# A graph layer on one core: half of the last block's tiles scattered into a matrix in the table stage, and shorter fills behind the scatters

## The chip, the cores and the metric

The kernel runs on one NeuronCore of a Trainium2 chip. The metric is the device time of one execution in microseconds (us). The time before is 271.71 us, the median of 3 runs (271.37 to 273.13). The engines are named as in the profile: PE is TensorE (matmul), PEld its weight load, DVE VectorE, ACT ScalarE, POOL GpSimd, SP SyncE. A q behind a name (SPq, ACTq) is an engine's instruction queue, from which DMAs are issued.

## The reference

One relational graph layer on 625 nodes of 512 features and 20,625 edges, sorted by destination. Each edge belongs to one of four relations and has a weight. In short:

```python
h = max(layernorm(x), 0)
total_msg = sum_r (h[src] @ W_rel[r] + b_rel[r]) * where(edge_type == r, edge_weight, 0)
agg = segment_sum(total_msg, dst) / max(segment_sum(edge_weight, dst), 1)
x1 = layernorm(h + h @ W_self + b_self + agg) * ln1_g + ln1_b
ffn = gelu(x1 @ W_ffn1 + b_ffn1) @ W_ffn2 + b_ffn2
out = x + layernorm(x1 + ffn) * ln2_g + ln2_b
```

All of it is float32.

## The kernel before

**Blocks and tiles.** The nodes lie in five blocks of up to 128 rows (`NB` = 5, the second has 113). The edges lie in 162 tiles of 128. From the counts alone (not the values) `EdgePlan` derives for each tile a window of rows in which its destinations must lie; a tile whose window leaves its block is kept for a slow way at the end, which counts show to be unused. Blocks 0 and 4 are the outer ones (`OUTER`): 31 tiles (0 to 30) lie wholly in block 0, and 32 (130 to 161) wholly in block 4.

**Table stage.** In 20 steps (4 relations by 5 blocks) `table_rows` makes the message of every node under every relation: eight matmul instructions a step on PE (L385), an eviction on DVE (L398), a store to the tensor `table` in HBM (L400). Some of these chunks stay on chip. Around the steps stand other works, each pinned to a step by a constant: the columns of the edges, one-hots for the degrees (`DEGREE_HOTS_AT`), the residual adds (`ADDS_AT`), the first hots for the banks (`HOTS_AT`). The order on PE, DVE, ACT and POOL is that of the program text.

**Edges of the outer blocks without gathers.** The tiles that lie wholly in an outer block are not gathered. Their contribution is a product: a matrix `sums_w[b]` of 128 nodes by 20 chunks by 128 rows holds the summed weights from each table row to each node of the block, and PE multiplies it with the 20 chunks of the table (`chunk_sum`, L1249). The matrix is made in two ways:

- Block 0, by scatter. The tiles' edges are loaded as a line with 63 neighbours on each side (`line`, L250). `line_columns` makes keys and places; `line_sums`, called for a piece of up to eight columns at the steps `COLUMNS_AT`, compares each edge with its neighbours (L639), keeps the first of each equal key and adds the weights of the others to it (L641 to L647). For each column, `scatter` then writes 128 weights to cells of the HBM tensor `cells`, cleared before (L256), with an indirect DMA on POOL (L653), and a memset (L656, 400 elements) as a fill behind it. `PACE` says how many scatters may be in the program by each step. `load_sums` loads the matrix back on ACT's queue (L670) at step `LOAD_AT`.
- Block 4, by banks. For each tile of the 32, `node_hots` makes two one-hots on DVE (L552 for two tiles at once, L562), `weighted_hots` two weighted copies on ACT (L570), and `outer_sum` two matmuls (L584) into a bank of PSUM that covers 25 nodes. A full bank is added to the overlap with the bank before (`empty_bank`, L525), copied (L536) and laid into `sums_w[4]` (L537). Three groups of two tiles are made in the table stage (`HOTS_AT`), the rest in the edge stage.

**Edge stage.** All other tiles, 99 of them, are gathered: an indirect DMA on POOL per tile (`gather`, L1103), each with a fill of 200 elements behind it (L1106); six more (L1161) fetch the edges at the borders of blocks. Eight buffers `ms` take the rows. ACT and DVE weight and add the rows (L1110, L1128), PE sums them by a one-hot (L1153). Then come the first norm, the feed-forward (L884, L902) and the second norm, block by block. The order on the engines is computed by a small planner (`Plan`) from costs in us that are written with each operation, with time zero near the end of the table stage and POOL free at 3.9.

**Between the stages on POOL.** At step `FIRST_AT` = 15, `load_first_edges` issues three indirect loads (L765), which `first_columns` on DVE reads later. `after_stores` (L663) is a short memset that waits for all table stores but the last two and for all scatters; the first gather stands behind it and waits for the last stores as well.

Of the kernel before, what the change touches and what calls it, by code (L numbers as in the profile page):

```python
# [20 lines left out]
PIECE = 8  # L21


class EdgePlan:
# [41 lines left out]
    def row(self, node):  # L66
        return node + (self.gap if node >= self.gap_at else 0)

# [80 lines left out]
def gnn_layer(ctx, tc, x, edges, edge_line, edge_groups, w_self, w_rel, w_ffn1, w_ffn2, rows_in, bf1_in, out, n_edges):  # L149
# [86 lines left out]
    LB, LJ, LN = outer[0]  # L236
    WL = LN + 2 * NEAR + 1
    line = early.tile([P, 4, WL], I32, name="line")
    cells = dram.tile([P * NC * P + P * LN, 1], F32, name="cells")

    def load_rows(to, n0, n1):
# [8 lines left out]
    nc.sync.dma_start(line, bass.AP(tensor=edge_line.tensor, offset=edge_line.offset,  # L250
                                    ap=[[LN, P], [edge_line.shape[1], 4], [1, WL]]))
# [4 lines left out]
    nc.sync.dma_start(cells[:P * NC * P, :].rearrange("(p c n) o -> p c (n o)", p=P, n=D // 2),  # L256
                      zeros.bitcast(F32).unsqueeze(1).to_broadcast([P, 2 * NC * P // D, D // 2]))
    nc.sync.dma_start(ed, edges)
    load_wr(1)
    load_rows(brel_bc[:, D:], D, R * D)  # L260
    load_rows(rows, R * D, (R + 6) * D)

    def later_loads(r):
        if r == 0:
            load_wr(2)
            nc.sync.dma_start(ws_sb, w_self)
            nc.sync.dma_start(bf1, bf1_in)
        if r == 1:
            load_wr(3)
            nc.sync.dma_start(w1_sb, w_ffn1)  # L270
        if r == 2:
            nc.sync.dma_start(w2_sb, w_ffn2)
# [170 lines left out]
    def count_outside():  # L443
# [8 lines left out]
        def total():  # L452
            pcnt = buffer("ps")
            nc.tensor.matmul(pcnt[0:1, 0:1], cnt, ones, start=True, stop=False)
            nc.tensor.matmul(pcnt[0:1, 0:1], x_missing, ones, start=False, stop=False)
            for i in range(2):
                nc.tensor.matmul(pcnt[0:1, 0:1], far[:, i:i + 1], ones, start=False, stop=(i == 1))
            return lambda: nc.vector.tensor_copy(n_out, pcnt[0:1, 0:1])
# [4 lines left out]
    banked_blocks = outer[1:]  # L463
    NE = sum(n for _, _, n in banked_blocks)

    GW = D // NC
    outer_tiles = [(b, j) for b, j0, n in banked_blocks for j in range(j0, j0 + n)]
# [42 lines left out]
    def empty_bank(k):  # L510
# [12 lines left out]
        def added():  # L523
            if not starts_:
# [3 lines left out]
        def copied():  # L528
            if starts_:
                for a, e in ((0, n0 - b * P), (max(bk[2] for bk in bank_of if bk[0] == b) - b * P, P)):  # L530
                    for a_ in range(a, e, GW):
                        n = min(GW, e - a_)
                        nc.scalar.activation(sums_w[b][:, :, a_:a_ + n], key_row[:, :NC * n].rearrange(
                            "p (c n) -> p c n", c=NC), AF.Copy, scale=0.0)
# [41 lines left out]
    def outer_sum(k, k0, box):  # L576
# [4 lines left out]
        for part in range(2):  # L581
# [5 lines left out]
    far = const.tile([P, 2], F32, name="far")  # L587
    spill = early.tile([P, LN], F32, name="spill")
    nc.gpsimd.iota(spill, pattern=[[1, LN]], base=P * NC * P, channel_multiplier=LN,
                   allow_small_or_imprecise_dtypes=True)  # L590
    place, found, weight = (early.tile([P, LN], F32, name=name) for name in ("place", "found", "weight"))
    cell = early.tile([P, LN], I32, name="cell")
    line_f = early.tile([P, 3, WL], F32, name="line_f")
    line_key = early.tile([P, WL], F32, name="line_key")
    own_of_line = slice(NEAR, NEAR + LN)
# [5 lines left out]
    def line_columns():  # L601

        own = own_of_line
        up = early.tile([P, 2, WL], F32, name="line_up")
        nc.vector.tensor_copy(line_f, line[:, 0:3, :])
        nc.vector.tensor_scalar(up, line_f[:, 0:2, :], float(ep.gap_at), float(ep.gap), op0=ALU.is_ge, op1=ALU.mult)
        nc.vector.tensor_add(line_f[:, 0:2, :], line_f[:, 0:2, :], up)
        s, d, t = line_f[:, 0, :], line_f[:, 1, :], line_f[:, 2, :]
        nc.vector.scalar_tensor_tensor(t, t, float(NP), s, op0=ALU.mult, op1=ALU.add)
        nc.vector.scalar_tensor_tensor(line_key, t, 1024.0, d, op0=ALU.mult, op1=ALU.add)  # L610
        part = early.tile([P, LN], F32, name="line_s")
        at = early.tile([P, LN], F32, name="line_t")
        e, near = nc.gpsimd, 1.5 * 2.0 ** 23
        e.tensor_scalar(found, d[:, own], float(LB * P), None, op0=ALU.is_ge)
        e.tensor_scalar(at, d[:, own], float(LB * P + P), None, op0=ALU.is_lt)
        e.tensor_mul(found, found, at)
# [3 lines left out]
        e.tensor_scalar(place, s[:, own], float(NC * P - 1), None, op0=ALU.mult)  # L620
        e.tensor_add(place, place, d[:, own])
        e.tensor_add(place, place, t[:, own])
        e.tensor_scalar(part, part, float(P - P * NC * P), float(-LB * P), op0=ALU.mult, op1=ALU.add)
        e.tensor_sub(part, part, spill)
        e.tensor_add(place, place, part)

    def line_check():
        d = line_f[:, 1, :]
        junk = early.tile([P, 2, LN], F32, name="line_j")
        for i, at in enumerate((2 * NEAR + 1, NEAR + 1)):  # L630
            nc.vector.scalar_tensor_tensor(junk[:, i, :], d[:, own_of_line], 0.0, d[:, at:at + LN], op0=ALU.add,
                                           op1=(ALU.is_equal, ALU.is_gt)[i], accum_out=far[:, i:i + 1])

    def line_sums(k0, k1):

        n, at = k1 - k0, slice(k0, k1)
        same = early.tile([P, PIECE, 2 * NEAR + 1], F32, tag="same", name=f"same_{k0}", bufs=1)[:, :n, :]
        own = line_key[:, NEAR + k0:NEAR + k1].unsqueeze(2).to_broadcast([P, n, 2 * NEAR + 1])
        nc.vector.tensor_tensor(same, sliding(line_key, k0, n, 2 * NEAR + 1), own, op=ALU.is_equal)  # L639
        earlier = early.tile([P, PIECE], F32, tag="earlier", name=f"earlier_{k0}", bufs=1)[:, :n]  # L640
        nc.vector.reduce_sum(earlier, same[:, :, :NEAR], axis=mybir.AxisListType.X)  # L641
        nc.vector.scalar_tensor_tensor(earlier, earlier, 0.0, found[:, at], op0=ALU.is_equal, op1=ALU.mult)
        nc.vector.tensor_mul(earlier, earlier, place[:, at])
        nc.vector.tensor_add(cell[:, at], earlier, spill[:, at])
        nc.vector.tensor_tensor(same[:, :, NEAR:], same[:, :, NEAR:],
                                sliding(line[:, 3, :].bitcast(F32), NEAR + k0, n, NEAR + 1), op=ALU.mult)
        nc.vector.reduce_sum(weight[:, at], same[:, :, NEAR:], axis=mybir.AxisListType.X)  # L647

    scattered = []
    idle = const.tile([P, 2 * PAUSE], BF16, name="idle")  # L650

    def scatter(k):
        i = nc.gpsimd.indirect_dma_start(  # L653
            out=cells[:, :], out_offset=bass.IndirectOffsetOnAxis(ap=cell[:, k:k + 1], axis=0),
            in_=weight[:, k:k + 1], in_offset=None)
        nc.gpsimd.memset(idle, 0.0)  # L656
        if scattered:
# [861 lines left out]
```

## Time and profile before

| what | value |
|---|---|
| median of 3 runs | 271.71 us |
| the profiled execution's own time | 273.46 us |
| its span, first to last instruction | 271.7 us |
| granted TensorE clock, mean | 0.987 |
| POOL busy | 202.9 us (75%), 378 instructions |
| DVE busy | 197.4 us (73%), 481 instructions |
| ACT busy | 75.3 us (28%), 182 instructions |
| PE busy | 255.7 us (94%), 1075 instructions |

All times in the profile are of one execution. PE's ends are modelled, so its busy share overstates it. A row of the time line gives the start, the duration, engine and line, operation, what is written and read, and in brackets the idle time of the engine ahead of it with what ended it. A row of the groups gives the busy sum, the mean in ns and the idle time in front. The chain of waits follows the work that ended last backwards, at each step to what released it.

### The profile page before, as it was taken

The numbers are of one execution on the slowest core, as the hardware profiler recorded it, in microseconds if no ns is written. First come the engines' busy times: TensorE is split into PE (matmuls) and PEld (weight loads), VectorE is DVE, ScalarE is ACT, GpSimd is POOL, SyncE is SP. The second block draws the span as 40 slices with busy tenths as digits, with TensorE's granted clock in tenths as the row PEclk, the third lists the DMA queues.
The fourth block names the chain that finished last, engine by engine and source line by source line (L and its number), as shares of the span: only waits on it lengthen the run. The fifth ranks groups of instructions, "written<-read, shape, count | busy, mean of one in ns | idle before, by whom it ended". The sixth has DMA issues, their size and how long they took to land.

```text
span 271.7 us, 3653 instructions
## 1 busy us (share of the span) xinstructions
PE 255.7 (94%) x1075; PEld 146.0 (54%) x1075; DVE 197.4 (73%) x481; ACT 75.3 (28%) x182; POOL 202.9 (75%) x378
## 2 busy tenths in 40 slices
PE   7799999999999979997799999999999998999993
PEld 5344444544547435552444345585684964856972
DVE  2877999869675955984885689784599975957514
ACT  3010000000130753875522123142133341520420
POOL 4789999999931888998898898888889898841000
PEclk9999999999999999999689999999999999999999
DMA  6999998712172886789659985666666577660101
GB/s 189 356 425 420 382 394 311 247 46 73 43 273 78 246 293 185 238 286 304 197 163 309 341 294 162 185 183 183 188 194 186 171 215 226 185 179 0 41 0 42
DMA packets 21495, 57.28 MB, mean 211 GB/s; under 512 B 3889, under 2 KB 6449, under 8 KB 20450
## 3 DMA queue, kind: packets, MB, share of 16 engines
q0 software_dynamic: 9488, 27.57, 34.5%
q1 hardware_dynamic: 11696, 28.02, 28.1%
q10 hardware_dynamic: 290, 1.44, 1.4%
q8 instruction: 9, 0.15, 0.2%
q14 instruction: 12, 0.10, 0.1%
HBM read 49.17 MB, written 7.85 MB: 210 GB/s over the span
## 4 chain that ended last, share of the span: by engine, by line
PE 35%; POOL 24%; DMA 21%; DVE 11%; issue 4%; ACT 1%; SPq 1%; POOLq 0%; DVEq 0%; ACTq 0%
PE ps L385 22%; DMA ms<-table,row_i 18%; POOL ms L1103 17%; POOL zeros L1106 5%; PE ps L902 4%; PE ps L884 3%; DMA wr<-in_L_gnn_W_rel_dram 2%; PE acc L1153 2%; POOL ms L1161 2%; DVE add L1128 2%; DVE es L1128 2%; PE acc L1249 1%; DVE z L1045 1%; DVE xs L1047 1%; DVE el L1118 1%
## 5 line engine op out<-in xcount | busy, mean ns | idle before, releaser
L1103 POOL DMA_INDIRECT ms<-table,row_i x99 | 101.3, 1023 | 18.7 <-issue 12.1
L385 PE MATMUL ps<-wr,hT 128*128 128x512 f32 (+2 forms) x168 | 71.3, 577 | 1.5 <-DMA wr<-in_L_gnn_W_rel_dram 1.5
L385 PEld LDWEIGHTS ps<-wr,hT 128*128 128x128 f32 x168 | 30.6, 190 | 35.5 <-issue 33.3
L1128 DVE SCALAR_TENSOR_TENSOR add<-ms,wgt_g,add 128x512 f32<-128x512 f32 x40 | 29.9, 749 | 16.5 <-DMA ms<-table,row_i 13.1
L884 PEld LDWEIGHTS ps<-x1T,w_sb 128*128 128x128 f32 x320 | 37.8, 192 | 4.0 <-issue 3.1
L653 POOL DMA_INDIRECT cells<-weight,cell x31 | 35.5, 1146 | 5.3 <-issue 4.8
L1110 ACT ACTIVATE add<-ms,ed 128x512 f32<-128x512 f32 x30 | 20.7, 691 | 64.4 <-DMA ms<-table,row_i 58.6
L884 PE MATMUL ps<-x1T,w_sb 128*128 128x128 f32 (+1 forms) x320 | 38.2, 275 | 0.1
L570 ACT ACTIVATE ohw<-os,w 128x128 fp32r<-128x128 f32 x64 | 19.8, 387 | 64.5 <-DVE os L552 64.2
L902 PE MATMUL ps<-w_sb,gT 128*128 128x512 f32 (+3 forms) x96 | 36.1, 522 | 0.0
L1249 PE MATMUL acc<-tr,sums_w 128*128 128x512 f32 x60 | 28.4, 592 | 0.0
L1106 POOL MEMSET zeros<- 128x200 bf16 x99 | 28.1, 283 | 0.1
L902 PEld LDWEIGHTS ps<-w_sb,gT 128*128 128x128 f32 (+1 forms) x96 | 16.6, 189 | 15.7 <-issue 13.5
L1153 PE MATMUL acc<-es,oh 128*128 128x512 f32 x40 | 22.1, 635 | 2.5 <-DVE es L1128 2.2
L1128 DVE SCALAR_TENSOR_TENSOR es<-ms,wgt_g,add 128x512 f32<-128x512 f32 x20 | 14.9, 744 | 7.8 <-DMA ms<-table,row_i 7.7
L410 PE MATMUL ps<-ws_sb,hT 128*128 128x512 f32 x40 | 20.3, 642 | 0.0
L584 PE MATMUL ps<-od,ohw 128*128 128x500 f32 (+16 forms) x64 | 16.0, 373 | 1.8 <-ACT ohw L570 1.8
L1249 PEld LDWEIGHTS acc<-tr,sums_w 128*128 128x128 f32 x60 | 10.9, 190 | 10.7 <-issue 10.5
L888 ACT ACTIVATE gT<-ps,bf 128x128 f32<-128x128 f32 (+1 forms) x40 | 13.2, 362 | 11.6 <-PE ps L884 11.1
L1167 DVE SCALAR_TENSOR_TENSOR z<-acc,rdeg,z 64x512 f32<-64x512 f32 (+1 forms) x13 | 9.7, 749 | 8.1 <-PE acc L1153 7.9
L584 PEld LDWEIGHTS ps<-od,ohw 128*128 128x128 f32 x64 | 10.4, 189 | 8.5 <-ACT ohw L570 6.0
L398 DVE SCALAR_TENSOR_TENSOR tr<-ps,rx,brel_bc 128x512 f32<-128x512 f32 x15 | 11.1, 741 | 4.4 <-PE ps L385 4.4
(201 smaller groups left out, 308.2 us busy)
## 6 DMA issues: line engine op xcount, KB each, us to landing
tr<-table SPq DMA_DIRECT2D x11, 512.0 KB, 5.5
w_sb<-in_L_gnn_W_ffn_dram SPq DMA_DIRECT2D x2, 2048.0 KB, 10.3
table<-tr SPq DMA_DIRECT2D x15, 256.0 KB, 4.3
wr<-in_L_gnn_W_rel_dram SPq DMA_DIRECT2D x3, 1024.0 KB, 7.5
ms<-table,row_i POOLq DMA_INDIRECT x99, 3.8
rows<-in_rows_dram SPq DMA_DIRECT2D x1, 1536.0 KB, 14.0
cells<-zeros SPq DMA_DIRECT2D x1, 1280.0 KB, 10.9
sums_w<-cells ACTq DMA_DIRECT2D x1, 1280.0 KB, 6.3
```

Of the source, the lines that this page charges most:

```text
L385: nc.tensor.matmul(p_[:, :h.stop - h.start], hT[i][:, k, :], wr_sb[r][:, k, h], start=(k == 0), stop=(k == KD - 1))
L410: nc.tensor.matmul(p[0], hT[i][:, k, :], ws_sb[:, k, :], start=(k == 0), stop=(k == KD - 1))
L584: nc.tensor.matmul(bank[b, n0][:, (lo - n0) * NC:(end - n0) * NC], box["ohw"][:, k - k0, part, :], box[k][:, :(end - lo) * NC], start=star ...
L653: i = nc.gpsimd.indirect_dma_start(out=cells[:, :], out_offset=bass.IndirectOffsetOnAxis(ap=cell[:, k:k + 1], axis=0), in_=weight[:, k:k + ...
L884: nc.tensor.matmul(pu[:, :nn], w1_sb[:, k, f * P:(f + 1) * P], x1T_b()[:, k, :nn], start=(k == 0), stop=(k == KD - 1))
L902: nc.tensor.matmul(po[h][:n, :w], box["gT"][:, f, at], w2_sb[:, f, c], start=(f == 0), stop=(f == KF - 1))
L1103: nc.gpsimd.indirect_dma_start(out=ms[j], out_offset=None, in_=table[:, :], in_offset=bass.IndirectOffsetOnAxis(ap=row_i[:, j:j + 1], axis=0))
L1106: nc.gpsimd.memset(zeros[:, :PAUSE], 0.0)
L1110: nc.scalar.activation(box["sum"], ms[j], AF.Copy, scale=wgt[:, j:j + 1])
L1128: nc.vector.scalar_tensor_tensor(to, ms[j], wgt_g[:, k, q - 1:q], box["sum"], op0=ALU.mult, op1=ALU.add)
L1153: nc.tensor.matmul(acc[bs], ohs[0][:, q, :].bitcast(F32), box["sum"] if "sum" in box else ms[j], start=(k == 0), stop=last)
L1249: nc.tensor.matmul(acc[b,], sums_w[b][:, c, :], kept[(b, c) if (b, c) in kept else c], start=first, stop=last)
```

## The change

The scatter way is made for a list of lines, (block, first tile, number of tiles): all 31 tiles of block 0, and the first 16 tiles of block 4 (130 to 145). The other 16 tiles of block 4 (146 to 161) stay with the banks, of which there are 4 in place of 10. Block 4's matrix comes from HBM with the scattered weights in it; the first bank is added to it where their nodes overlap, and the copies that filled the rest of the matrix with zeros are gone.

```diff
+LINES = 999, 16
+    def lines(self):
+        outer = [(b, [j for j, bs in enumerate(self.blocks) if bs == [b]]) for b in (0, len(self.first) - 1)]
+        return [(b, t[0], min(len(t), most)) for (b, t), most in zip(outer, LINES)]
...
+    def clear_cells(i):
+        nc.sync.dma_start(cells[i][:P * NC * P, :].rearrange("(p c n) o -> p c (n o)", p=P, n=D // 2),
+                          zeros.bitcast(F32).unsqueeze(1).to_broadcast([P, 2 * NC * P // D, D // 2]))
...
+    load_line(0)
...
+    clear_cells(0)
     nc.sync.dma_start(ed, edges)
     load_wr(1)
+    load_line(1)
     load_rows(brel_bc[:, D:], D, R * D)
     load_rows(rows, R * D, (R + 6) * D)
...
         if r == 0:
             load_wr(2)
+            clear_cells(1)
             nc.sync.dma_start(ws_sb, w_self)
...
-    banked_blocks = outer[1:]
+    banked_blocks = [(b, j0 + m, n - m) for (b, j0, n), (_, _, m) in zip(outer, lines) if n > m]
...
-        starts_ = b not in sums_w
+        starts_ = not sums
         if starts_:
-            sums_w[b] = const.tile([P, NC, P], F32, name=f"sums_w{b}")
-            both = n0
+            both = min(n1, max(n0, scattered_to))
...
         def added():
-            if not starts_:
+            if starts_:
+                if both > n0:
+                    nc.vector.tensor_add(t[:, :(both - n0) * NC].rearrange("p (n c) -> p n c", c=NC),
+                                         p[:, :(both - n0) * NC].rearrange("p (n c) -> p n c", c=NC),
+                                         sums_w[b][:, :, n0 - b * P:both - b * P].rearrange("p c n -> p n c"))
+            else:
                 nc.vector.tensor_add(t[:, :(both - n0) * NC], p[:, :(both - n0) * NC],
                                      t_[:, (n0 - m0) * NC:(both - m0) * NC])
...
-        nc.gpsimd.memset(idle, 0.0)
+        nc.gpsimd.memset(idle[:, :PAUSE // 2], 0.0)
...
-    PRE = 3
-    ADDS_AT, HOTS_AT = (12, 13, 14), (15, 16, 17)
+    ADDS_AT, HOTS_AT = (13, 15, 16), (17,)
...
-    PACE = 3
+    PACE = 3.4
+    CELLS = 3.0
-    COLUMNS_AT, DEGREE_HOTS_AT = (0, 2, 4, 9, 12), (7, 8, 10, 11)
+    COLUMNS_AT, LINE_AT, DEGREE_HOTS_AT = (0, 2, 4, 9, 11, 12, 14), 10, (7, 8, 10, 11)
...
-        line_columns()
+        line_columns(0, nc.gpsimd)
...
+                if step == LINE_AT:
+                    line_columns(1, nc.vector)
                 if step in COLUMNS_AT:
                     next_columns()
-                while columns and len(scattered) < PACE * (step + 1):
-                    scatter(columns.pop(0))
+                while columns and sum(len(s) for s in scattered) < PACE * (step + 1):
+                    scatter(*columns.pop(0))
                 if step == LOAD_AT:
-                    load_sums()
+                    load_sums(0)
...
+    landed = op("cells", CELLS, None)
-    banked, before_ = [], None
+    banked, before_ = [op("ACT", 0.1, lambda: load_sums(1), after=[landed], lag=7.5, rank=(0, 0))], None
```

`PAUSE` is 200, so the fill behind a scatter has 100 elements in place of 400. There are 47 scatters in place of 31. The columns of the second line are made wholly on DVE at step 10 (the small ones of the first line are on POOL), its two pieces of eight columns at steps 12 and 14. The second matrix is loaded by ACT's queue in the edge stage, after all of its scatters but the last have landed; the planner takes 3.0 us after its time zero for that. The check of the lines (`line_check`) is made for both.

More of the change, by code (lines that the diff above doesn't have):

```diff
@@ L619, in line_columns @@
         e.tensor_scalar(part, part, -near, None, op0=ALU.add)
[L620 to L640, printed above, removed]
+        e.tensor_scalar(to, s[:, own], float(NC * P - 1), None, op0=ALU.mult)
```

179 lines of the change are left out of this document (102 added, 77 removed).

## The prediction

> **What bounds the kernel now.** I read the chain of waits first, then the costliest groups, then the time line of GpSimd (POOL), and only then VectorE's (DVE) and TensorE's (PE).
>
> ```profile
> PE 35%; POOL 24%; DMA 21%; DVE 11%; issue 4%; ACT 1%; SPq 1%; POOLq 0%; DVEq 0%; ACTq 0%
> ...
> L1103 POOL DMA_INDIRECT ms<-table,row_i x99 | 101.3, 1023 | 18.7 <-issue 12.1
> L1106 POOL MEMSET zeros<- 128x200 bf16 x99 | 28.1, 283 | 0.1
> ```
>
> The chain has two halves: PE at the table's products, then POOL and its gathers. The time line says where they meet.
>
> ```profile
> 18.33 1.28 POOL L653 DMA_INDIRECT cells<-weight,cell  x1 [0.34 <-DVE weight L647]
> 19.62 0.45 POOL L656 MEMSET idle<- 128x400 bf16 x1
> ...
> 23.43 1.11 POOL L326 TENSOR_TENSOR rx<-rx,half 128x1 f32<-128x1 f32 x1
> ...
> 73.98 1.00 POOL L765 DMA_INDIRECT x_edges<-in_edge_groups_dram,x_group  x1 [0.16 <-issue]
> 75.29 1.14 POOL L765 DMA_INDIRECT x_edges<-in_edge_groups_dram,x_group  x1 [0.30 <-issue]
> 76.73 0.94 POOL L765 DMA_INDIRECT x_edges<-in_edge_groups_dram,x_group  x1 [0.30 <-issue]
> 84.33 0.10 POOL L663 MEMSET idle<- 128x2 bf16 x1 [6.65 <-issue]
> 87.27 0.95 POOL L1103 DMA_INDIRECT ms<-table,row_i  x1 [2.84 <-DVE x_step L773]
> ...
> 88.66 0.95 POOL L1103 DMA_INDIRECT ms<-table,row_i  x1 [0.16 <-issue]
> ...
> 128.51 0.95 POOL L1103 DMA_INDIRECT ms<-table,row_i  x1 [0.16 <-issue]
> ...
> 239.88 0.95 POOL L1103 DMA_INDIRECT ms<-table,row_i  x1 [0.16 <-DVE ow L927]
> ```
>
> From the first scatter at 18.33 to the last edge load at 77.67 POOL never rests; then it idles until the table is stored, and the first gather starts at 87.27. Between 77.67 and 87.27 lie 9.6 us of slack, the only room that POOL has. From there to the 105th gather at 239.88 it issues without a break: 152.6 us, of which 104 steps of 1.39 us (88.66 - 87.27) make 144.6 and stalls some 8. What follows is a fixed tail of 31.8 us (271.7 - 239.88). So the end is the first gather's start, plus 105 gathers, plus the tail; no gather is added or removed.
>
> **The scatters.** There are 31 now and 47 after. All 47 come ahead of the three edge loads in POOL's order, because the pacing has released them by step 14 and the edge loads come at step 15.
>
> ```profile
> L653 POOL DMA_INDIRECT cells<-weight,cell x31: 964/988/1861, 18.3 to 72.4; - x31
> ...
> L653 POOL DMA_INDIRECT cells<-weight,cell x31 | 35.5, 1146 | 5.3 <-issue 4.8
> ```
>
> Undisturbed, one scatter takes 0.96 us, a gap of 0.17 (5.3 / 31) and the fill. The fill of 400 elements takes 0.45, that of 200 takes 0.28, that of 2 takes 0.10. For 100 I interpolate 0.20 (an estimate, between 0.10 and 0.28). The undisturbed step falls from 1.58 to 1.33, and 47 steps are 62.5 us. An edge load without any fill follows the one before after 1.31 and 1.44 us, so a scatter is not held at the old step merely because its fill is short.
>
> The mean of 1.146 against 0.964 is 0.18 of stall per scatter, 5.6 us in all. These rows show where it comes from:
>
> ```profile
> 27.63 1.21 DVE L639 TENSOR_TENSOR same<-line_key 128x1016 f32<-128x1016 f32 x1
> ...
> 27.97 1.70 POOL L653 DMA_INDIRECT cells<-weight,cell  x1 [0.17 <-issue]
> ...
> 50.61 1.18 DVE L731 TENSOR_TENSOR oc<-rel,row_w 128x988 bf16<-128x988 bf16 x1
> ...
> 50.76 1.86 POOL L653 DMA_INDIRECT cells<-weight,cell  x1 [0.17 <-issue]
> ```
>
> Both scatters end 0.83 us after the DVE operation with two SBUF inputs beside which they began (29.67 - 28.84, 52.62 - 51.79): they stand until it is over. The change adds such operations. Two pieces of eight columns each bring one like L639 (1.2 us) and a shorter one at L645. An operation of length d catches a scatter in a share d/1.5 of cases and holds it d/2, so 0.48 + 0.15 for each piece; with the columns' own operations about 1.5. The old 5.6 grow to 6.7 at the denser step. I take 8.2, between 5 and 12.
>
> Of the Trainium skill, the page "SBUF — State Buffer", section "Who interferes with whom", says that a DVE instruction with two SBUF inputs contends with a GpSimd instruction that reads SBUF, which is what these rows show. The same section infers that such a DVE operation does not hold descriptor generation; the two rows above differ, and the measurement decides. By that inference the added pieces would cost the scatters nothing; it is the second rival.
>
> POOL's sum: 18.33 + 1.1 (the square root at 23.43) + 62.5 + 8.2 = 90.1. The three edge loads take 3.7 (73.98 to 77.67): 93.8. With the marker of 0.1 and a gap, the first gather starts at 94.0, 6.7 us later than now. The marker also waits for the last scatter to land:
>
> ```profile
> cells<-weight,cell POOLq DMA_INDIRECT x31, 5.1
> sums_w<-cells ACTq DMA_DIRECT2D x1, 1280.0 KB, 6.3
> ```
>
> The last scatter starts about 88.6 and lands at 93.7, beside the edge loads, so this adds nothing. The bounds of this term: 5 us of stalls and a fill of 0.10 give 85.9 (then the table decides); 12 and a fill of 0.28 give 101.4. Both ends need every part at its worst; within the forecast I hold 92 to 96.5.
>
> **DVE and PE in the table stage.** The change moves work into steps 10 to 14: all of the second line's columns on DVE at step 10, pieces at 11, 12 and 14, the residual adds from 12 to 14 to 13, 15 and 16; two of the three early hot groups leave steps 15 and 16.
>
> ```profile
> L644 DVE TENSOR_TENSOR cell<-earlier,spill 128x8 int32<-128x8 f32 (+2 forms) x5 | 0.8, 165 | 0.2
> ...
> 8.51 0.41 DVE L605 CAST line_f<-line 128x474 f32<-128x474 int32 x1
> ...
> 10.19 0.32 DVE L610 SCALAR_TENSOR_TENSOR line_key<-line_f 128x158 f32<-128x158 f32 x1
> ...
> 46.20 1.20 DVE L639 TENSOR_TENSOR same<-line_key 128x1016 f32<-128x1016 f32 x1
> ...
> 49.95 0.74 DVE L398 SCALAR_TENSOR_TENSOR tr<-ps,rx,brel_bc 128x512 f32<-128x512 f32 x1
> ...
> 56.45 0.75 DVE L398 SCALAR_TENSOR_TENSOR tr<-ps,rx,brel_bc 128x512 f32<-128x512 f32 x1 [2.61 <-PE ps L385]
> 57.12 0.55 DVE L639 TENSOR_TENSOR same<-line_key 128x381 f32<-128x381 f32 x1
> ...
> 59.22 0.74 DVE L1045 SCALAR_TENSOR_TENSOR z<-z,rx,rows 128x512 f32<-128x512 f32 x1
> ...
> 61.75 0.74 DVE L398 SCALAR_TENSOR_TENSOR tr<-ps,rx,brel_bc 128x512 f32<-128x512 f32 x1
> ...
> 64.93 0.87 DVE L794 COPY dg<-add 4x512 f32<-4x512 f32 x2
> ...
> 67.67 0.06 DVE L801 MEMSET counts<- 128x4 f32 x1
> ...
> 68.11 0.16 DVE L806 TENSOR_REDUCE rdeg<-ps 128x5 f32<-128x15 f32 x1
> ...
> 65.66 0.47 PE L799 MATMUL ps<-ident,dg 4*128 4x4 f32 x5 [0.37 <-DVE dg L794]
> ...
> 69.59 0.28 PE L758 MATMUL ps<-counts,before 128*128 128x3 f32 x2
> ```
>
> A piece of eight costs 3.75 (46.20 to 49.95), of three 2.1 (57.12 to 59.22), the adds of two blocks 2.53 (59.22 to 61.75), an eviction 0.66, the degree copies 0.73 (64.93 to 65.66). The second line's columns: five wide operations like those from 8.51 to 10.51, 2.0 less a tenth for the shorter line, and twelve small ones on 16 columns, at 0.17 by the row of L644 (8 columns), so 3.9 (between 3.0, if independent ones overlap, and 4.5). I chain them from the eviction of step 10 at 49.95: + 0.66 + 3.9 + 1.1 (a degree one-hot, 1.18 at 50.61 with its end under the next) = 55.6; + 0.66 + 2.1 + 1.1 = 59.5 for step 11; + 0.66 + 3.75 = 63.9 for step 12; + 0.66 + 2.53 + 0.73 = 67.8 for step 13. PE's transposes of the degrees waited 0.37 for these copies and ran at 65.66; now they run at 67.8, 2.1 late. Then 0.66 + 3.75 (the piece of step 14) + 0.45 (67.67 to 68.11) gives the counts at 72.7, and PE's L758 stands for them: 3.1 late against 69.59. The table would end, and the first gather could start, at 87.27 + 3.1 = 90.4. POOL at 94.0 hides this; it is the floor if POOL is faster than I think.
>
> On SP's queue the second line's load stands ahead of the bias rows and the second clearing (1280 KB) ahead of the self weights.
> ```profile
> L385 PE MATMUL ps<-wr,hT 128*128 128x512 f32 (+2 forms) x168 | 71.3, 577 | 1.5 <-DMA wr<-in_L_gnn_W_rel_dram 1.5
> ...
> cells<-zeros SPq DMA_DIRECT2D x1, 1280.0 KB, 10.9
> ```
>
> PE's products wait 1.5 us in all for transfers, and the first scatter into the second matrix comes after step 12, past 56.45, tens of us behind a clearing issued after the fifth product; so both cost nothing. Without that cover the clearing would cost at most its 10.9.
>
> **The gather stage.** 16 of 32 banked tiles leave, and so do the hot groups' two-input operations:
>
> ```profile
> L552 DVE TENSOR_TENSOR os<-key,node_row x16: 402/408/418, 70.5 to 125.4; 128x256 f32<-128x256 f32 x16
> ```
>
> Of 16 groups three were made early and 13 ran beside gathers; after, 8 less one made early leaves 7. From 87.27 to 128.51 are 27 steps, 37.5 us at 1.39 in 41.2: stalls of 3.7, some 3.3 of them at such groups, 0.25 each. Six fewer save 1.5 us (between 0 and 3.3). The rest of the removed bank work (DVE, ScalarE, PE) lies beside POOL's issue and saves nothing by itself.
>
> The wait added: the load of the second matrix stands on ScalarE's queue until the last-but-one scatter has landed, about 93, with weighted hots and the gathers' first rows behind it; the first row is due only when gathers have landed, about four us after 94. It lands at 99.3 (6.3), and DVE's first bank addition waits for it. I take nothing for both.
>
> **Sum:** + 6.7 - 1.5 = + 5.2. The profiled execution took 273.46 (span 271.7, 1.8 around it), so it becomes 278.7; the median, 271.71, lies 1.75 below that execution and becomes 276.9. Alone this case reaches from 275 to 279.5.
>
> **Rivals.** (1) POOL catches up and the table's end decides: + 3.1 - 1.5 = + 1.6, 273.3. For it: a fill nearer 0.10 and stalls near 5. Against it: the extra work falls where DVE is busiest. (2) Faster: a scatter takes 0.96 whatever DVE does, the wide pieces do not hold it, and POOL is free at 18.33 + 1.1 + 62.5 + 3.7 = 85.6, below 87.27; if DVE also keeps PE on time and all 3.3 us of bank stalls go, 268.4. It decides if POOL's edge loads end before the last table store. The rows at 27.97 and 50.76 speak against it. (3) DVE's first columns wait for the edge loads (at 86.36 now; about 97 then), four us more than the gathers slip, and bank sums behind them keep gather buffers from coming free: the ninth gather waits and the four us stay, 281. It decides if POOL shows waits over 0.2 us ahead of a gather. Against it: half the bank work is gone. (4) The short fill does nothing and the step stays at 1.76: 47 steps are 82.7, first gather at 106, about 289.
>
> **Chances.** Forecast 0.62, (1) 0.15, (2) 0.06, (3) 0.13, (4) 0.04. The range, 272.6 to 280.5, takes in (1), its gather term up to 0.7 better, and goes halfway from the forecast's own end to (3); about 0.17 is left out. One per cent, 2.7 us, is what can be told from no change: faster than 269.0 is (2), 0.06; within 269.0 to 274.4 is (1) and the forecast's edge, 0.19; slower 0.75.
>
> **What would show it.** POOL: 47 scatters at a step near 1.5, the last edge load ending about 93.8 with no idle ahead of the first gather at 94. PE: degree transposes about two us late. Gathers: stalls to the 28th down to about 2.2 us. I am wrong if POOL still idles before the first gather, or if a gather waits for a buffer.

## The result, and the profile after

| | before | after |
|---|---|---|
| median | 272.19 us (270.02 to 275.89, 6 runs) | 279.97 us (279.27 to 280.58, 6 runs) |
| ratio to before | 1 | 1.030, 95% interval 1.027 to 1.034 |
| profiled execution, its span | 273.46, 271.7 us | 280.58, 278.8 us |
| first gather | 87.27 | 100.94 |
| first to last gather | 152.6 | 147.0 |
| from the last gather to the end | 31.8 | 30.9 |

The change is 3.0% slower: 7.1 us of span, which are 13.7 lost ahead of the first gather, 5.6 won in the gather stage and 1.0 in the tail. The prediction, 276.9, lay 3.1 us below the median and had the sign. Of its steps not all held. The executions of a kernel can fall into a faster and a slower group; ratios here and below are of the faster ones, and where a kernel has too few of them none is given.

The page after: the chain of waits by engine, then two groups (busy us, mean ns | idle us ahead and its cause).

```profile
DVE 23%; PE 22%; POOL 22%; DMA 21%; issue 8%; SPq 1%; ACT 0%; POOLq 0%; DVEq 0%; ACTq 0%
...
L673 POOL DMA_INDIRECT cells<-weight,cell x47 | 51.5, 1097 | 8.8 <-issue 7.5
...
L1277 PE MATMUL acc<-tr,sums_w 128*128 128x512 f32 x60 | 28.7, 612 | 4.8 <-DMA sums_w<-cells 4.8
```

Two things show at once. The mean scatter takes 1.097 us, 0.133 over the undisturbed 0.964, where the prediction's 8.2 us over 47 had 0.174. And the chunk sums, which waited for nothing of note before, now wait 4.8 us for the load of a scattered matrix. POOL's time line after (start, duration, operation, idle time ahead with its cause):

```profile
18.87 1.28 POOL L673 DMA_INDIRECT cells<-weight,cell  x1 [0.78 <-DVE weight L667]
...
88.33 0.20 POOL L676 MEMSET idle<- 128x100 bf16 x1
88.68 1.24 POOL L786 DMA_INDIRECT x_edges<-in_edge_groups_dram,x_group  x1 [0.16 <-DVE os L568]
90.22 0.95 POOL L786 DMA_INDIRECT x_edges<-in_edge_groups_dram,x_group  x1 [0.30 <-issue]
91.48 0.94 POOL L786 DMA_INDIRECT x_edges<-in_edge_groups_dram,x_group  x1 [0.30 <-issue]
98.66 0.10 POOL L688 MEMSET idle<- 128x2 bf16 x1 [6.24 <-DMA table<-m]
100.94 1.03 POOL L1131 DMA_INDIRECT ms<-table,row_i  x1 [2.19 <-DVE os L568]
...
139.02 0.95 POOL L1131 DMA_INDIRECT ms<-table,row_i  x1 [0.16 <-issue]
...
247.94 0.95 POOL L1131 DMA_INDIRECT ms<-table,row_i  x1 [0.16 <-DVE oh L1167]
```

The fill takes the 0.20 that was interpolated, and the edge loads end at 92.42 (93.8 was forecast). But POOL then idles twice, 6.24 and 2.19 us, and the first gather waits for table stores. POOL's string of scatters became as long as forecast and did not decide; the table did. PE's time line tells why, of before and then of after:

```profile
66.06 3.70 PE L385 MATMUL ps<-wr,hT 128*128 128x512 f32 x8
...
70.41 14.02 PE L385 MATMUL ps<-wr,hT 128*128 128x512 f32 x40
84.26 1.02 PE L1249 MATMUL acc<-tr,sums_w 128*128 128x512 f32 x2
```

```profile
67.37 0.41 PE L820 MATMUL ps<-ident,dg 4*128 4x4 f32 x4 [1.46 <-DVE dg L815]
72.61 2.05 PE L1277 MATMUL acc<-tr,sums_w 128*128 128x512 f32 x2 [4.83 <-DMA sums_w<-cells]
74.58 0.27 PE L820 MATMUL ps<-ident,dg 4*128 4x4 f32 x1
74.78 5.00 PE L402 MATMUL ps<-wr,hT 128*128 128x512 f32 x8
79.62 0.28 PE L779 MATMUL ps<-counts,before 128*128 128x3 f32 x2
...
80.43 14.02 PE L402 MATMUL ps<-wr,hT 128*128 128x512 f32 x40
```

Before, the first chunk sum ran at 84.26, behind the last table product. After, one chunk sum of block 0 stands between the fourth and the fifth transpose of the degrees, and PE, which here takes its instructions in order, stands there for 4.83 us until block 0's matrix has come back from HBM. This matrix was loaded from 74.86 before; now its load is issued at 65.90, and the order on PE has the product ahead of 48 table products (8 and 40) that have nothing to do with it. The order of the program text holds within the table stage and within the edge stage; this product is written in the edge stage, and its place among the products of the table stage shows only in the trace. That the earlier load is what moved it is borne out by the run with the long fill below. The granted clock fell too:

```profile
60.00:67.00 7.00, 5.92 (x71) 3.07 (x69) 6.83 (x13) 0.00 (x0) 6.17 (x11) 1.00 0.32 94
67.00:76.00 9.00, 3.80 (x9) 1.71 (x10) 5.71 (x24) 0.00 (x0) 8.01 (x13) 0.70 0.48 167
76.00:81.00 5.00, 5.00 (x18) 2.56 (x17) 1.18 (x2) 0.00 (x0) 4.44 (x8) 0.86 0.02 2
```

(Stretch, then the busy time of PE, its weight loads, DVE, ACT and POOL, then the granted clock.) The stretch of the stand has 0.70; cut finer, the clock is 1.00 from 67.0 to 70.0, 0.62 to 72.6 and 0.50 to 76.0. The eight products behind the stand took 5.00 us in place of 3.70, and the chunk sum itself 1.97 where two such products had 1.02 before. From the transposes to step 16 (its products are the first of the x40) are 13.06 us (67.37 to 80.43) against 4.75 (65.66 to 70.41): 4.83 of wait, 1.97 for the chunk sum (72.61 to 74.58), 1.30 of slower products, 0.21 of rest. With 1.71 that the transposes came late, the table's last product ends 10.0 us later, at 94.45 (80.43 + 14.02) against 84.43.

The other 3.65 us lie between the last product and the first gather, 6.49 against 2.84. First the times from issue to landing, over the stretch from 88 to 102 of after; then the row that before had in its own list; then the load's issue and the last store's in the time line of after:

```profile
sums_w<-cells ACTq DMA_DIRECT2D x1, 1280.0 KB, 6.6
...
table<-m SPq DMA_DIRECT2D x1, 192.0 KB, 5.7
```

```profile
table<-m SPq DMA_DIRECT2D x1, 192.0 KB, 1.9
```

```profile
90.73 0.33 ACTq L693 DMA_DIRECT2D sums_w<-cells  x1
...
94.86 1.14 SPq L417 DMA_DIRECT2D table<-m  x1
```

The second matrix, 1280 KB, is under way from 90.73 for 6.6 us, and one of the last stores into the table, for which the gathers stand, takes 5.7 us where it took 1.9. Of the 3.65 us, 0.82 lie ahead of the end of the last store's issue (1.55 us after the last product, against 0.73), and 2.83 between that and the first gather (4.94 against 2.11).

One reading needs care. The page puts the first gather's last wait down to DVE, and the chain of waits leads from the edge loads through DVE's first columns to it. If the gather needed those columns, it would start behind the same DVE operation everywhere. It does not: after the change it starts behind the last of them (100.38, 0.17 long), in an experiment below 0.04 us behind the first (96.79, 0.18 long, against a gather at 97.01). In every trace it comes behind the last table store, by the times in the table further down.

### The profile page after: what moved, and what is told of

Read it like the earlier page. It is cut to its first block, busy times and chain, and to the rows that moved or that the text cites. A ratio compares the mean times of both kernels' runs of the same rounds, so it can differ in the third digit from the quotient of the medians.

```text
span 278.8 us, 3590 instructions
## 1 busy us (share of the span) xinstructions
PE 251.6 (90%) x1047; PEld 141.6 (51%) x1047; DVE 198.6 (71%) x487; ACT 62.4 (22%) x138; POOL 208.5 (75%) x411
## 4 chain that ended last, share of the span: by engine, by line
DVE 23%; PE 22%; POOL 22%; DMA 21%; issue 8%; SPq 1%; ACT 0%; POOLq 0%; DVEq 0%; ACTq 0%
POOL ms L1131 12%; DMA ms<-table,row_i 11%; PE ps L402 9%; POOL zeros L1134 4%; POOL cells L673 4%; PE acc L1277 3%; PE acc L1181 3%; DMA ms<-table,x_row 3%; DVE add L1156 3%; PE ps L905 3%; PE ps L923 2%; DMA sums_w<-cells 2%; DMA line<-in_edge_line_dram 2%; DMA x_edges<-in_edge_groups_dram,x_group 1%; DVE tr L415 1%
## 5 line engine op out<-in xcount | busy, mean ns | idle before, releaser
L1131 POOL DMA_INDIRECT ms<-table,row_i x99 | 96.2, 972 | 18.0 <-issue 11.6
L402 PE MATMUL ps<-wr,hT 128*128 128x512 f32 (+2 forms) x168 | 72.5, 585 | 1.3 <-DMA wr<-in_L_gnn_W_rel_dram 1.3
L673 POOL DMA_INDIRECT cells<-weight,cell x47 | 51.5, 1097 | 8.8 <-issue 7.5
L402 PEld LDWEIGHTS ps<-wr,hT 128*128 128x128 f32 x168 | 31.1, 193 | 36.0 <-issue 30.9
L586 ACT ACTIVATE ohw<-os,w 128x128 fp32r<-128x128 f32 x32 | 10.2, 390 | 81.0 <-DVE os L568 73.5
L1181 PE MATMUL acc<-es,oh 128*128 128x512 f32 x40 | 20.9, 603 | 1.7 <-DVE es L1156 1.5
L427 PE MATMUL ps<-ws_sb,hT 128*128 128x512 f32 x40 | 18.7, 595 | 0.0
L909 ACT ACTIVATE gT<-ps,bf 128x128 f32<-128x128 f32 (+1 forms) x40 | 13.6, 363 | 16.7 <-PE ps L905 13.7
L1181 PE MATMUL acc<-ms,oh 128*128 128x512 f32 x18 | 10.7, 706 | 4.5 <-POOL zeros L1134 4.5
L1181 PEld LDWEIGHTS acc<-es,oh 128*128 128x128 f32 x40 | 7.0, 189 | 9.7 <-DVE es L1156 5.3
```

Source lines behind the costliest of these rows:

```text
L402: nc.tensor.matmul(p_[:, :h.stop - h.start], hT[i][:, k, :], wr_sb[r][:, k, h], start=(k == 0), stop=(k == KD - 1))
L427: nc.tensor.matmul(p[0], hT[i][:, k, :], ws_sb[:, k, :], start=(k == 0), stop=(k == KD - 1))
L673: s = nc.gpsimd.indirect_dma_start(out=cells[i][:, :], out_offset=bass.IndirectOffsetOnAxis(ap=cell[i][:, k:k + 1], axis=0), in_=weight[i] ...
L1131: nc.gpsimd.indirect_dma_start(out=ms[j], out_offset=None, in_=table[:, :], in_offset=bass.IndirectOffsetOnAxis(ap=row_i[:, j:j + 1], axis=0))
L1181: nc.tensor.matmul(acc[bs], ohs[0][:, q, :].bitcast(F32), box["sum"] if "sum" in box else ms[j], start=(k == 0), stop=last)
```

## Experiments

Two theories came out of the traces. **A:** PE's early chunk sum made the table late. **B:** the second matrix's load delays the last table stores. The rival, from the prediction: POOL's string and the gather stage decide, whatever PE does.

All later runs fell on chips where every kernel, the one before too, was slower (medians of before 283 to 287 us). So times are compared on one chip only, and mechanisms by stretches of the trace.

**A alone, B alone, both, and the fill alone (one chip).** For A the first chunk sum is ordered behind the last table product:

```diff
+                last_product[:] = [nc.tensor.matmul(p_[:, :h.stop - h.start], hT[i][:, k, :], wr_sb[r][:, k, h],
+                                                    start=(k == 0), stop=(k == KD - 1)).ins]
...
+        m = nc.tensor.matmul(acc[b,], sums_w[b][:, c, :], kept[(b, c) if (b, c) in kept else c], start=first, stop=last)
+        if first and b == OUTER[0]:
+            tc.add_manual_dep(m.ins, last_product[0].name, mybir.DependencyInfo(
+                mybir.DependencyClass.NoSync, mybir.DependencyReason.DATA), reason="behind the table")
```

> The changed kernel, with the first chunk sum of block 0 (L1277) held behind the last table product in PE's order and nothing else moved. Theory (PE stands 4.83 us at this chunk sum for the load of the first matrix, in the middle of the degree transposes, runs slow behind the stand, and the late table end then meets the second matrix's load): the transposes end near 67.7, the table's last eviction near 87.7 in place of 94.5, the last stores land ahead of the second load, and POOL's edge loads (end 92.4) decide: first gather near 93 in place of 100.94, of which 1 to 2 us are given back by bank hots that then run beside gathers. Time 273 to 274.5. Rival (the work moved on DVE is what makes the table late, and the chunk sum only fills the wait): the table ends at most 3 us earlier, 277 or more. Rival (the scatters on POOL decide, as forecast): no change, 280.

For B the second load also waits for the last two stores:

```diff
-                 scattered[i][:-1], "all cells are there")
+                 [*scattered[i][:-1], *(stored if i else [])[-2:]], "all cells are there")
```

> The changed kernel, with the load of the second matrix (L693) made to wait also for the last two table stores, so that it doesn't run beside them; the chunk sum stays where it is. Theory: the last stores land in 2 us in place of 6, the first gather starts near 97.3 in place of 100.94, time 276 to 277; the matrix lands near 104, and DVE's first bank addition waits for it without reaching the gathers. Rival (the stores are slow for another reason): the first gather stays at 100 to 101, time 279 to 281.

Both edits:

> Both edits. Theory: with the chunk sum held, the last stores land before the second matrix's load can start (its scatters land at 90.7), so the second edit adds nothing: 273 to 274.5, as with the chunk sum held alone. If the two were independent the gains would add: 269 to 270.

The kernel before with the short fill (`idle[:, :PAUSE // 2]`) and nothing else:

> The kernel before with the shorter fill alone (100 in place of 400 elements behind its 31 scatters). Theory: POOL reaches its idle stretch 7.9 us earlier (31 x 0.25) and waits there for the table as now: same time as before, within 0.5 us, first gather at 87.3. Rival (the shorter fill lets scatters disturb the table's loads and stores): slower by 1 us or more.

Measured, against before at 285.22 us: A alone 1.041 (1.028 to 1.054), B alone 1.031 (1.020 to 1.041), both 1.025 (1.012 to 1.039), the fill alone 289.57 (283.99 to 291.46), with no ratio. The intervals overlap; the totals do not tell the edits apart, and the forecast that A alone would bring the time back to that of before failed. The traces tell more. With A:

```profile
73.72 0.47 PE L821 MATMUL ps<-ident,dg 4*128 4x4 f32 x5
74.12 3.70 PE L403 MATMUL ps<-wr,hT 128*128 128x512 f32 x8
78.89 0.39 PE L780 MATMUL ps<-counts,before 128*128 128x3 f32 x2 [1.07 <-DVE counts L827]
79.80 14.02 PE L403 MATMUL ps<-wr,hT 128*128 128x512 f32 x40
```

The chunk sum is gone from between the transposes, and from there to step 16 are 6.08 us, not 13.06. But A's absolute times missed: PE reached the transposes only at 73.72, because its degree sums, 2 us before, stood again and again. With B alone PE was as late, at 72.94. It came to the chunk sum at 73.27, 7.3 us after the first load's issue at 65.99, and did not wait there at all; its stretch was 6.07 as well. So in this trace of A there was nothing left to take away: the 1.1 us of the chunk sum came back as 1.07 of wait for DVE's counts. What B did is in the time lines of SP's and ACT's queues and of POOL:

```profile
94.70 0.32 SPq L417 DMA_DIRECT2D table<-m  x1
95.11 0.38 SPq L1272 DMA_DIRECT2D tr<-table  x1
```

```profile
96.40 0.33 ACTq L693 DMA_DIRECT2D sums_w<-cells  x1
```

```profile
93.51 0.10 POOL L688 MEMSET idle<- 128x2 bf16 x1 [0.44 <-issue]
97.01 0.95 POOL L1131 DMA_INDIRECT ms<-table,row_i  x1 [3.40 <-DVE x_cols L792]
```

The marker, which stood 6.24 us in the changed kernel, stands 0.44, and the gather follows the last store's issue by 2.0 us. The other transfers close to it, the reloads of table rows (`tr`), are where they were, so they are not what delays the stores. With the fill alone, the scatters end at 65.43, POOL then has 14 us of idle time, and the first gather (94.28) follows the table's last product by 2.74 us, against 2.84 in the kernel before: in this trace a faster POOL alone does not bring the gather nearer to the table's end.

**The same again, and fewer tiles (another chip).** A and B once more; and A with `LINES = 999, 12`, which scatters 12 tiles and leaves 20 to the banks (the fill's buffer is cut to the 100 elements in use, so that the larger banks fit).

> The chunk sum held, once more: on the chip of the first set every kernel, the one before too (285), stood up to some 3 us at a time with nothing that the profile names as cause, the degree sums of the table stage among them. Theory on a chip without such stands: transposes near 67.7, last eviction near 87.7, POOL's edge loads (end 92.4) decide, first gather near 93, ratio to the kernel before 1.000 to 1.010. Rival (the work moved on DVE makes the table late, the chunk sum only fills the wait): ratio 1.02 or more. Rival (the store's collision with the second load is all): no change, 1.030.

> The second load held behind the last table stores, once more, the chunk sum where the change has it. In the first set its first gather came 4.0 us after the last table product against 6.4 with the chunk sum held alone. Theory: PE stands 4.8 us at the chunk sum as in the changed kernel, the last stores land in some 2 us in place of 6, first gather near 97.5 in place of 100.94, ratio 1.015 to 1.020. Rival (the collision costs nothing): 1.030.

> The chunk sum held, and 12 tiles in place of 16 scattered to the second matrix (20 by banks); the fill's buffer is cut to its size to make room. Theory: four scatters fewer take 5.5 us (at 1.38) from POOL, its edge loads end near 87, and the second piece on DVE is shorter by 1.6, so the table decides again: last eviction near 86.5, first gather near 89.5; the gathers' stalls save 2 to 4 of the old 8.0. Ratio 0.99 to 1.00. Rival (POOL isn't what decides once the chunk sum is held): the same as the chunk sum held alone.

Against 286.58: A 1.038 (1.032 to 1.044), B 301.66 with no ratio, A with 12 tiles 1.016 (1.008 to 1.023). A's forecast (1.000 to 1.010) failed again, and so did that for 12 tiles (0.99 to 1.00); A's ratio lies where the rival about DVE had it, but PE reached the transposes only at 82.00, so this run does not decide between the two. In that last run's profile the degree sums did not stand, and PE came to the transposes as early as in the changed kernel:

```profile
62.32 3.70 PE L403 MATMUL ps<-wr,hT 128*128 128x512 f32 x8
68.28 0.47 PE L821 MATMUL ps<-ident,dg 4*128 4x4 f32 x5 [2.25 <-DVE dg L816]
68.68 3.70 PE L403 MATMUL ps<-wr,hT 128*128 128x512 f32 x8
72.22 0.28 PE L780 MATMUL ps<-counts,before 128*128 128x3 f32 x2
...
73.02 14.02 PE L403 MATMUL ps<-wr,hT 128*128 128x512 f32 x40
```

This is the cleanest sight of A, though the edit to 12 tiles is in it too. The first matrix's load was issued at 68.03 here; at 6.6 us to land, an early chunk sum would have stood until about 74.6 (worked out, not run). Held back, it lets PE go from the transposes to step 16 in 4.74 us, as before the change, and the table ends at 87.04 in place of 94.45. With 12 tiles DVE's last piece is shorter too, so the wait for the counts is gone. The kernel is still 1.6% slower than before, and its first gather, at 93.34, is 6.1 us later: 2.6 us because DVE brings PE to the transposes late, 3.2 between the last product and the end of the last store's issue (3.91 against 0.73; the last two evictions on DVE stood 2.08 us of it, with a cause that was not tried), and only 0.3 from there to the gather.

**A control, and both edits once more (a third chip).** The changed kernel itself, both edits with 16 and with 12 tiles, and the long fill put back (`nc.gpsimd.memset(idle, 0.0)`).

> The changed kernel itself once more, beside the kernels of this call on one chip. Theory (the first chunk sum stands 4.83 us among the degree transposes; the second matrix's load runs beside the last table stores): 1.030 times the kernel before, from the last four-transpose group to step 16 13 us, from the last table product to the first gather 6.5 us. Rival (a chance of the one profiled execution): another stand and another ratio. On a chip where the PE reaches the transposes late, after 72 us, the load of the first matrix has landed by then, and the chunk sum's wait would be under 1 us with the same order of instructions; the stretch to step 16 would then be 7 to 8 us.

> Both causes taken away with 16 tiles still scattered: the first chunk sum behind the last table product, the second matrix's load behind the last two table stores. Theory: transposes to step 16 about 6 us, last table product to first gather 3 to 4 us; the first gather is some 8 us earlier than in the changed kernel where the PE stood the 4.8 us, 3 to 4 us earlier where it did not; but the 47 scatters on POOL still end the edge loads at 92 us, so no earlier than 92.4 + 1.5 = 94: ratio 1.005 to 1.015. Rival (POOL and the gather stage decide whatever the two do): ratio as the changed kernel beside it, within 0.5%.

> Both causes taken away and 12 tiles scattered in place of 16 (the fill's buffer cut to the 100 elements that are used). Theory: table's end near 87 as with the hold and 12 tiles alone, then 3 to 4 us to the first gather where that run had 6.3, so a first gather at 90 to 91 and a ratio 1.010 below that run's 1.016: 1.00 to 1.01. Rival (what is lost is paid in the gather stage, by the two more banks to fetch): the first gather comes earlier but the ratio stays at 1.016.

> The changed kernel with the fills behind its 47 scatters at 400 elements again. If POOL has 6 us to spare ahead of the first gather, as the changed kernel's trace shows, the longer fills cost what exceeds it: 47 x 0.25 = 12 us at the step of 1.4 to 1.6 that the kernel before had, so edge loads end at about 104 and the first gather lies at about 105, 4 us behind the changed kernel's 101, with no idle time of POOL ahead of the gather. Rival (the loads and stores behind the table stage decide alone): first gather still at 101.

Medians, with before at 283.33: the changed kernel 299.0, both edits 297.72, both with 12 tiles 288.46, the long fill 302.57 in a single execution; no ratio is given. The lowest times were 277.75 before, 297.41 changed, 286.79 with both edits and 282.97 with both and 12 tiles. That goes the way of the theory, but these are single executions without a profile and show no cause. The changed kernel's PE on this chip:

```profile
62.13 0.48 PE L769 MATMUL add<-oc,w 128*4 128x2 bf16 x13
63.81 0.22 PE L769 MATMUL add<-oc,w 128*4 128x9 bf16 x2 [1.20 <-issue]
65.23 0.22 PE L769 MATMUL add<-oc,w 128*4 128x5 bf16 x2 [1.20 <-issue]
...
84.42 0.41 PE L820 MATMUL ps<-ident,dg 4*128 4x4 f32 x4
84.75 1.12 PE L1277 MATMUL acc<-tr,sums_w 128*128 128x512 f32 x2
85.81 0.22 PE L820 MATMUL ps<-ident,dg 4*128 4x4 f32 x1
```

The order is that of the first profile, with the chunk sum between the transposes, but PE comes 17 us later and the chunk sum does not wait: the second case of the expectation, though the stretch to step 16 was 6.06 us, not 7 to 8. This shows that the 4.83 us are a race between PE and a load. From the last table product to the first gather are 6.52 us, as forecast. The lateness costs something else in its place:

```profile
75.13 0.96 POOL L673 DMA_INDIRECT cells<-weight,cell  x1 [0.17 <-issue]
76.09 0.20 POOL L676 MEMSET idle<- 128x100 bf16 x1
89.31 0.96 POOL L673 DMA_INDIRECT cells<-weight,cell  x1 [13.02 <-DVE counts L822]
```

POOL stands 13.02 us ahead of its last eight scatters. Their weights come from DVE's piece at step 14, which stands in DVE's order behind an eviction that waits for PE. Through the pieces at late steps the change has made POOL's string depend on PE's progress; where PE is on time, this costs nothing, where it is late, the delay goes on into the edge loads (ended at 104.6).

Both edits, with 16 and with 12 tiles, met the same lateness (first gathers at 105.89 and 102.83), so their forecasts of absolute times missed. The stretch from the transposes to step 16 was 6.07 and 4.75.

The long fill missed both theories' numbers. Its scatters ended later, so the first matrix was loaded at 77.13 in place of 65.90, the chunk sum waited 7.89 us for it, and the second load, issued at 103.22, fell wholly beside the last store:

```profile
69.16 0.52 PE L820 MATMUL ps<-ident,dg 4*128 4x4 f32 x5 [3.18 <-DVE dg L815]
69.61 5.29 PE L402 MATMUL ps<-wr,hT 128*128 128x512 f32 x8
82.79 2.04 PE L1277 MATMUL acc<-tr,sums_w 128*128 128x512 f32 x2 [7.89 <-DMA sums_w<-cells]
```

```profile
105.05 0.95 POOL L786 DMA_INDIRECT x_edges<-in_edge_groups_dram,x_group  x1 [0.30 <-issue]
105.99 0.12 POOL L688 MEMSET idle<- 128x2 bf16 x1
113.56 0.95 POOL L1131 DMA_INDIRECT ms<-table,row_i  x1 [7.45 <-DVE x_cols L795]
```

The five transposes stand together here, and the chunk sum comes behind eight more products. Only the fill differs from the changed kernel, so the place of the chunk sum in PE's order moves with the time at which its matrix is loaded. Even with POOL busy until 106, the first gather waits 7.45 us more. The length of the scatter string acts through the loads that wait for it.

**Both edits, a last time (a fourth chip).**

> The kernel with both causes taken away and 16 tiles scattered, once more. If the PE's degree sums run without stands (2 us for the last group, as in the changed kernel's first profile), the theory gives: degree transposes at 67.4, step 16 six us later or less at 72 to 74, table's end near 87.5, the last three edge loads ended by POOL at 92.4 as in the changed kernel, so POOL late by then and no idle time over 2 us ahead of the first gather at 94; ratio 1.005 to 1.015, against 1.030 for the changed kernel. Rival: the first gather stays at 100 or the ratio at 1.03, and something not yet seen holds it. If the degree sums stand again (the last group over 10 us), the table's end is late from that alone and only the stretches tell: transposes to step 16 6 us, last table product to first gather 3 to 4 us.

Against 286.55: 1.035 (1.024 to 1.046). The degree sums stood for about 4 us (the transposes at 73.16), so neither of the two cases of the expectation was met in full. The stretches came as A and B say, 6.07 us to step 16 and 2.1 from the last store to the first gather, but that gather lies at 97.81, not 94, and the ratio is no better than the changed kernel's own. The gather stage took 160.7 us there. With the fill alone it took 160.6 and with A alone 158.6, on one chip: on these chips single gathers wait up to 5.0 us (both edits, first chip) behind operations of ACT, DVE and PE (3.0 in the kernel without the second matrix), where the first two profiles have none over 0.2 us.

**B over all traces.** From the end of the last table store's issue to the first gather, with the issue of the second load:

| trace | second load issued | last store's issue ended | first gather | between |
|---|---|---|---|---|
| before (no second load) | | 85.16 | 87.27 | 2.1 |
| changed kernel | 90.73 | 96.00 | 100.94 | 4.9 |
| the same, third chip | 102.16 | 105.24 | 111.02 | 5.8 |
| long fill | 103.22 | 103.75 | 113.56 | 9.8 |
| A | 90.77 | 96.58 | 100.25 | 3.7 |
| A again | 100.07 | 105.32 | 108.54 | 3.2 |
| A, 12 tiles | 85.27 | 90.95 | 93.34 | 2.4 |
| B | 96.40 | 95.02 | 97.01 | 2.0 |
| B again | 103.95 | 102.19 | 104.56 | 2.4 |
| A and B, three runs | 101.18, 105.28, 97.20 | 99.34, 103.89, 95.74 | 101.80, 105.89, 97.81 | 2.5, 2.0, 2.1 |
| A and B, 12 tiles | 102.22 | 100.83 | 102.83 | 2.0 |

Where the load is issued 5.2 to 5.9 us ahead of the end of the last store's issue, 2.4 to 4.9 us pass; where it is issued 3.1 us ahead, 5.8; where 0.5 us ahead, 9.8. In these six traces the first gather comes 8.1 to 10.3 us behind the issue of the load. Where the load comes behind the store, the interval is that of the kernel before within 0.4 us, six times of six. B is shown for this interval. A is shown as a mechanism (the wait in the first profile; the stretch with it held back; no wait where the load had landed). That A and B together would bring the changed kernel to 1.005 to 1.015 on a chip like the first is not shown: no later run fell on one. On the later chips the kernel with both edits was still 2.5 and 3.5% slower than the one before; what makes up the rest is open, since the kernel before has no profile there beyond the one with the short fill.

## Why the prediction was right, and where not

- **POOL's string** (+ 6.7, edge loads at 93.8). Right in size: 92.42, with the fill at 0.20, and some 6.2 us of stalls (0.133 x 47) for 8.2. Wrong in its role: "POOL at 94.0 hides this" failed. POOL idled 8.4 us, and the text had named that as a sign of being wrong.
- **DVE and PE in the table stage** (transposes at 67.8, counts + 3.1, floor at 90.4). The transposes came at 67.37, so the chain of DVE durations held to 0.4 us. The floor was 10.5 us too low. The step that failed is the list of what stands on PE up to step 16: it had the transposes and the counts, and not the chunk sum, because the edge stage's first products were taken to stand behind the table, as they did before. With its matrix loaded 9 us earlier, the first of them came ahead of step 16, waited 4.83 us there and slowed the products behind it.
- **The wait added** ("I take nothing for both"). This asked who waits for the second load, which was right: the first bank addition hid it. It did not ask what the load runs beside: the last stores into the table. The stretch there grew by 3.65 us, of which 2.83 lie behind the last store's issue, where the runs show the load as the cause; the other 0.82 were not tried.
- **Rival (1)**, that the table's end decides, named the right place at + 3.1; it was + 13.7.
- **Gather stage** (- 1.5). Mis-sized: - 5.6, and - 1.0 in the tail. Up to the 28th gather 38.08 us (100.94 to 139.02) against 41.24 make 3.2 of it. With the gathers late, the two-input operations of five bank groups, not of one, ran ahead of them, so ten fewer ran beside them, not six. The other 2.4 came later, where the prediction had looked for nothing: what the gathers took above the undisturbed 0.95 us fell from 4.1 to 1.6 us behind the 28th (from 3.4 to 0.2 up to it). Why it fell there was not tried.
- **The sum** held because errors cancel: first gather + 6.9 against the forecast, gather stage - 4.1, tail - 1.0, in all + 1.9 (before rounding) on the profiled execution (280.58 against 278.7). The number was near for the wrong reason.
- **Scatters and two-input DVE operations.** The rows at 27.97 and 50.76 carried the estimate of stalls, and the mean after agrees with it to a quarter. After the change the scatters at 66.06, 67.92, 82.44 and 85.64 again ended 0.84 to 0.86 us after a DVE operation with two SBUF inputs (L659, L1072). But those at 64.73 and 81.10 took the undisturbed 0.96 and 0.97 us beside one that started 0.03 and 0.05 us after them, so which scatters are held, and with it the share in the estimate, stays open. The Trainium skill's inference to the contrary, in "SBUF — State Buffer", "Who interferes with whom", would have had POOL free at about 86 (rival 2); it was 92.4.

## What to carry to other kernels

When a load is moved earlier, look at which products it sets free: an engine that works in order may now meet them ahead of work that everything waits for, and stand there for the load's last microseconds. When a large transfer is added, ask not only who waits for it but which small transfers on the path it will run beside. And an engine that is busy longer delays the end only if what it releases is the last to come: for the engine next in line, write down the earliest possible end with all that stands in its queue.

## What was not expected of the hardware

- After a stand of 4.83 us PE's granted clock was 0.70 over a 9 us stretch, and eight products took 5.00 us in place of 3.70. On the later chips products behind the standing degree sums were slow likewise: eight took 6.28 us (at 67.51 with A), with a clock of 0.79 from 60 to 76. The Trainium skill, "TensorE: Matmul & The Clock Gate", Part 1, says that the gate falls to half rate after about one idle window of 3.4 us; the stand of 4.83 us and the clock of 0.50 from 72.6 to 76.0 agree.
- A store of 192 KB took 5.7 us to land beside a load of 1280 KB, 1.9 without it (one trace each).
- On the later chips, in most profiles, PE stood some 0.5 to 1.9 us between every few of its small degree sums, with no cause that the profile names ("issue"), in the kernel before with the short fill as well; the last group grew from 2 to up to 17 us. What does it stays open.
